# A second GpSimd drain in the last stage of an attention and mixture-of-experts kernel

## The chip, the cores and the metric

The kernel runs on one NeuronCore of a Trainium2 chip. The metric is the device time of one execution in microseconds. Before the change the median of three runs is 1449.51 us (1448.92 to 1450.37). Beside these stands one execution under the hardware profiler, from which all durations below come.

## What is computed

The reference is a post-norm transformer block over `x` of shape (4, 1024, 256): attention with 16 heads of size 16 and rotary-like position factors, a residual and a layer norm, then a mixture of 8 experts with top-2 routing and a capacity, a residual and a second layer norm. Only the second half matters here:

```python
logits = x_flat @ router_w + router_b
gates = softmax(logits)
_, topk_idx = top_k(gates, 2)
expert_mask = one_hot(topk_idx, 8).sum(1)
pos = cumsum(expert_mask, axis=0) - 1          # the token's slot within its expert
expert_mask = expert_mask * (pos < capacity)   # capacity = 640 slots for each of 8 experts
buf[e, pos] += x_flat                          # tokens are dispatched to slots
h = gelu(einsum('ecd,edh->ech', buf, w1) + b1[:, None, :])
out = einsum('ech,ehd->ecd', h, w2) + b2[:, None, :]
y = sum over e of out[e, pos] * gates
x = layernorm(x + y)
```

There are N = 4096 tokens of 256 features; an expert's hidden width is 1024.

## The kernel before

**Attention** takes the first 1130 us or so. It is a hand-written order of pieces over 32 units (batch, head group) and is not touched. While it runs, GpSimd scatters every finished token's row into the table `slots_in` in DRAM (L646), twice per tile of 128 tokens, one row for each of its two experts.

**The expert stage** begins at L1056. It is a loop over the experts `e` from 0 to 7 (L1206), within `tc.manual_schedule()`, so that the order of the source is the order of each engine's queue. An expert's 640 slots are five tiles of 128 (`ST` = 5). For each expert:

- SP loads the slots of the next expert (L1210), and the VectorE works out for the slots which token each belongs to, its gate, and three row numbers (`tokens_of`, L1085).
- GpSimd gathers five tiles of partial results that an earlier expert left for the same tokens (`others_of`, L1168, one indirect transfer per tile).
- If there was an expert before, its rows, which are now complete for those tokens that have no later expert, are normalized (`normalized`, L1220) and scattered to the output by GpSimd (`sent`, called at L1224, the transfer is L1191), one indirect transfer per tile. Rows that are not finished have a row number beyond the bounds and are skipped by the transfer.
- First layer: eight groups of four matmuls (L1230), each followed by a Gelu on ScalarE (L1237).
- Second layer: for each of the five tiles eight matmuls (L1249). For experts 0 to 6 the result is biased, weighted, added to the row and scattered to the table `y_rank` (L1267). For the last expert it is added to the row (L1257), the row is normalized by itself (L1260) and sent to the output at once (L1261, the transfer is again L1191).

All these indirect transfers are issued from GpSimd, which writes their descriptors itself; SP and ScalarE issue plain ones. GpSimd's queue is strictly in order. Each transfer signals its landing on one of eight semaphores in turn. `out_views` (L1188) gives the first tile of each expert a view of the whole output, so the scatter of the second tile waits for the landing of the first.

**The end of the program** is written by the framework when the `TileContext` closes, so it has the line L1344: SP waits for the last value of every semaphore, that is, for every landing and every engine. Then all five engines meet: each executes a `DRAIN` and signals, GpSimd waits for the other four, releases them, drains again, clears the semaphores, and there is a second meeting of the same kind. The program has no GpSimd drain between the meeting at its start (L1332) and this one.

Of the kernel before, what the change touches and what calls it, by code (L numbers as in the profile page):

```python
# [28 lines left out]
def kernel(  # L29
# [18 lines left out]
    nc = tc.nc  # L48
    B, S, DIM = x.shape
    E, _, HID = w1.shape  # L50
# [41 lines left out]
    def expert_weights(e):  # L92
        w_sb = big.tile([P, 4, S], F32, tag="big", name=f"w_{e}")
        w1_sb = w_sb[:, 0:2, :]
        nc.sync.dma_start(w1_sb, w1[e].rearrange("(k p) f -> p k f", p=P))
        w2_sb = w_sb[:, 2:4, :].rearrange("p k (c d) -> p (k c) d", d=DIM)
        nc.sync.dma_start(w2_sb, w2[e].rearrange("(k p) d -> p k d", p=P))
        return w1_sb, w2_sb
# [3 lines left out]
    with ExitStack() as actx:  # L102
# [869 lines left out]
        with tc.manual_schedule():  # L972
            for n in range(NS):
                u, c = divmod(n, NT)
                b, p = divmod(u, NU)
                if c == 0:
                    if u + 2 < B * NU:
                        load_qk(u + 2)
                    elif u + 2 - B * NU < 2:
                        e = u + 2 - B * NU  # L980
# [75 lines left out]
    with ExitStack() as mctx:  # L1056
# [12 lines left out]
        def slots_of(e):  # L1069
            s_sb = m2.tile([P, ST, ROW], F32, tag="slots", name=f"slots_{e}")  # L1070
            nc.sync.dma_start(
                s_sb, slots_in[e * CAP : (e + 1) * CAP, :].rearrange("(t p) d -> p t d", p=P)
            )
            return s_sb

        def transposed(e, s_sb, t):

            if t == 0:
                s_ts[e] = m2.tile([P, KC, CAP], F32, tag="slots_t", name=f"slots_t_{e}")
            ps = ps_t.tile([P, KC, P], F32, tag="t", name=f"st_{e}_{t}")  # L1080
            for k in range(KC):
                nc.tensor.transpose(ps[:, k, :], s_sb[:, t, k * P : (k + 1) * P], ident)
            nc.scalar.copy(s_ts[e][:, :, t * P : (t + 1) * P], ps)  # L1083

        def tokens_of(e, s_sb):  # L1085


            mine = m2.tile([P, 2, ST, 2], F32, tag="mine", name=f"mine_{e}")
            w = m2.tile([P, ST], F32, tag="w", name=f"w_{e}")
            gone = m2.tile([P, 3, ST], F32, tag="gone", name=f"gone_{e}")  # L1090
            to = m2.tile([P, 3, ST], U32, tag="to", name=f"rows_{e}")
            nc.vector.tensor_scalar(
                mine[:, 0], s_sb[:, :, DIM + 2 : DIM + 4], float(E - e), None, ALU.is_equal
            )
            nc.vector.tensor_tensor(mine[:, 1], mine[:, 0], s_sb[:, :, DIM : DIM + 2], ALU.mult)
            nc.vector.tensor_reduce(w, mine[:, 1], AX.X, ALU.add)
            nc.vector.tensor_reduce(gone[:, 0], mine[:, 0], AX.X, ALU.add)
            nc.vector.tensor_tensor(gone[:, 0], gone[:, 0], s_sb[:, :, DIM + 4], ALU.mult)
            nc.vector.tensor_scalar(gone[:, 0], gone[:, 0], -1.0, NOWHERE, ALU.mult, ALU.add)
            for i, k in ((1, 1), (2, 0)):  # L1100
                nc.vector.scalar_tensor_tensor(
                    gone[:, i], mine[:, 0, :, k], float(N), gone[:, 0], ALU.mult, ALU.add
                )

            nc.vector.tensor_scalar(gone[:, 2], gone[:, 2], 2.0 * N - 1.0, None, ALU.min)
            nc.vector.tensor_copy(to, gone)
            return w, to
# [44 lines left out]
        def without_experts(q):  # L1152


            t0 = q * NQ
            for t in range(t0, t0 + NQ):
                nc.vector.tensor_scalar(x1[:, t, :], x1[:, t, :], again[:, t : t + 1], None, ALU.mult)
            b, t = divmod(t0, NT)
            nc.sync.dma_start(
                out[b, t * P : (t + NQ) * P, :].rearrange("(t p) d -> p t d", p=P),  # L1160
                x1[:, t0 : t0 + NQ, :],
            )
# [27 lines left out]
        def sent(row, to, t):  # L1190
            nc.gpsimd.indirect_dma_start(  # L1191
                out=out_views[t],
                out_offset=bass.IndirectOffsetOnAxis(ap=to[:, 0, t : t + 1], axis=0),
                in_=row[:, t, :],
                in_offset=None,
                bounds_check=N - 1,
                oob_is_err=False,
            )
# [4 lines left out]
        with tc.manual_schedule():  # L1203
            for t in range(ST):
                transposed(0, tiles[0], t)
            for e in range(E):  # L1206
                w1_sb, w2_sb = experts.pop(e)
                s_sb, s_t = tiles.pop(e), s_ts.pop(e)
                if e + 1 < E:
                    tiles[e + 1] = slots_of(e + 1)  # L1210
                if e == 0:
                    for q in range(7, 3, -1):
                        without_experts(q)
                w, to = tokens_of(e, s_sb)
                others = others_of(e, s_sb, w, to)
                row = next(others)

                if before:
                    b_row, b_to = before
                    normalized([b_row[:, t, :] for t in range(ST)], f"e_{e}")  # L1220
                next(others, None)
                if before:
                    for t in range(ST):
                        sent(b_row, b_to, t)  # L1224
                h_t = m2.tile([P, HC, CAP], F32, tag="h", name=f"h_{e}")
                for c in range(HC):
                    ps = ps_h.tile([P, 2, 512], F32, tag="h", name=f"hp_{e}_{c}")
                    for k in range(KC):
                        for i in range(2):
                            nc.tensor.matmul(  # L1230
                                ps[:, i, 0:half],
                                w1_sb[:, k, c * P : (c + 1) * P],
                                s_t[:, k, i * half : (i + 1) * half],
                                start=(k == 0),
                                stop=(k == KC - 1),
                            )
                    nc.scalar.activation(  # L1237
                        h_t[:, c, :].rearrange("p (i n) -> p i n", i=2),
                        ps[:, :, 0:half],
                        AF.Gelu,  # L1240
                        bias=b1_sb[:, e, c : c + 1],
                    )
                for t in range(ST):
                    if e + 1 < E and t > 0:
                        for i in (t - 1,) if t < ST - 1 else (t - 1, t):
                            transposed(e + 1, tiles[e + 1], i)
                    ps = ps_o.tile([P, DIM], F32, tag="o", name=f"op_{e}_{t}")
                    for c in range(HC):
                        nc.tensor.matmul(  # L1249
                            ps,  # L1250
                            h_t[:, c, t * P : (t + 1) * P],
                            w2_sb[:, c, :],
                            start=(c == 0),
                            stop=(c == HC - 1),
                        )
                    if e == E - 1:
                        nc.vector.scalar_tensor_tensor(  # L1257
                            row[:, t, :], ps, w[:, t : t + 1], row[:, t, :], ALU.mult, ALU.add
                        )
                        normalized([row[:, t, :]], f"e_{e}_{t}", by_scalar=True)  # L1260
                        sent(row, to, t)  # L1261
                        continue
                    o_sb = m4.tile([P, DIM], F32, tag="o", name=f"o_{e}_{t}")
                    nc.vector.tensor_tensor(o_sb, ps, b2_sb[:, e, :], ALU.add)  # L1264
                    nc.scalar.activation(o_sb, o_sb, AF.Identity, scale=w[:, t : t + 1])  # L1265
                    nc.vector.tensor_tensor(row[:, t, :], row[:, t, :], o_sb, ALU.add)
                    nc.gpsimd.indirect_dma_start(  # L1267
                        out=y_views[e * ST + t],
                        out_offset=bass.IndirectOffsetOnAxis(ap=to[:, 1, t : t + 1], axis=0),
                        in_=o_sb,  # L1270
                        in_offset=None,
                        bounds_check=2 * N - 1,
                        oob_is_err=False,
                    )
                    if e == 0 and t < 4:
                        without_experts(3 - t)
                before = row, to
                if e + 2 < E:
                    experts[e + 2] = expert_weights(e + 2)
# [68 lines left out]
```

## Time and profile before

| | |
|---|---|
| median of 3 runs | 1449.51 us |
| the profiled execution, its time | 1455.47 us |
| the profiled execution, its span (first to last instruction) | 1453.6 us |
| granted TensorE clock, mean | 0.972 |
| busy: PE, VectorE, ScalarE, GpSimd | 94%, 63%, 50%, 28% of the span |
| indirect transfers from GpSimd | 64 (L646), 40 (L1191), 35 (L1267), 35 (L1168) |
| descriptor work of one L1191 transfer on GpSimd | 0.98 us in the median |
| distance of the last five L1191 transfers | 3.45 us |

The time of the profiled execution is 1.87 us longer than its span, and 5.96 us longer than the median of the runs. Times in the profile are counted from the first instruction. An entry with a `q` behind the engine's name (POOLq, SPq) was executed by that engine's queue and is not part of its busy time: waits, register moves, semaphore instructions and drains. The engine names PE, DVE, ACT and POOL stand for TensorE, VectorE, ScalarE and GpSimd.

### The profile page before, as it was taken

The page shows a single profiled execution, that of the slowest core. Times are in us where ns is not written, and L with a number is a line of the kernel's source. Part 1 is how long each engine was busy: PE and PEld are TensorE (multiplying, and loading weights), DVE is VectorE, ACT ScalarE, POOL GpSimd, SP SyncE. Part 2 cuts the span into 40 slices and gives each one's busy share as a digit, 9 for nine tenths or more (in the row PEclk, how much of TensorE's full clock was granted, in tenths as well). Part 3 has the DMA queues.
Part 4 walks back from the last instruction along what each step waited for, and adds up shares of the span by engine and source line. Part 5 has one row for each costly group of instructions (what it writes and reads, how often), then busy time and mean ns, then how long its engine had stood idle before and what let it go on. Part 6 is the DMA issues. An engine that isn't in the chain of part 4 may idle for free. (4 is left out here: it accounts for less than half of the span.)

```text
span 1453.6 us, 24361 instructions
## 1 busy us (share of the span) xinstructions
PE 1367.7 (94%) x9314; PEld 859.4 (59%) x9314; DVE 921.3 (63%) x1990; ACT 727.5 (50%) x944; POOL 411.2 (28%) x436
## 2 busy tenths in 40 slices
PE   5899999999999999999999999999996399999996
PEld 3455555655665565555555555555543277777775
DVE  7767766667877766787767677887644433333334
ACT  5365666565566556546674654655553122222221
POOL 5640043340002637000064530000210414444542
PEclk8899999999999999999999999999998599999998
DMA  7956367373444646454465352224210436433211
GB/s 240 261 177 173 100 188 205 87 228 107 126 120 113 213 133 180 121 151 102 129 185 181 105 176 74 63 63 118 90 64 0 139 112 212 115 120 131 73 44 43
DMA packets 107315, 191.23 MB, mean 132 GB/s; under 512 B 19633, under 2 KB 56178, under 8 KB 107072
## 3 DMA queue, kind: packets, MB, share of 16 engines
q1 hardware_dynamic: 96192, 167.80, 39.7%
q0 software_dynamic: 9888, 20.01, 4.5%
q10 hardware_dynamic: 1120, 1.87, 0.4%
q8 instruction: 73, 1.20, 0.4%
q14 instruction: 42, 0.34, 0.1%
HBM read 119.32 MB, written 73.63 MB: 133 GB/s over the span
## 5 line engine op out<-in xcount | busy, mean ns | idle before, releaser
L705 DVE TENSOR_REDUCE nm<-s 128x1 f32<-128x512 f32 x1024 | 644.8, 684 | 230.4 <-PE s L701 212.6
L750 ACT ACTIVATE pt<-st 128x1024 f32<-128x1024 f32 x512 | 496.3, 1021 | 393.7 <-PE st L743 378.9
L701 PE MATMUL s<-qk 128*128 128x512 f32 x1024 | 391.5, 441 | 25.6 <-DVE nm L705 14.5
L728 PE MATMUL st<-qk 128*128 128x512 f32 x1024 | 308.4, 401 | 3.5 <-ACT pt L750 3.4
L764 PE MATMUL av<-pt,va 128*32 128x256 f32 x4096 | 275.5, 386 | 0.5 <-ACT pt L750 0.5
L701 PEld LDWEIGHTS s<-qk 128*128 128x128 f32 x1024 | 180.2, 191 | 138.3 <-DVE nm L705 62.4
L728 PEld LDWEIGHTS st<-qk 128*128 128x128 f32 x1024 | 183.3, 189 | 67.1 <-ACT pt L750 32.7
L764 PEld LDWEIGHTS av<-pt,va 128*32 128x32 f32 x4096 | 107.1, 109 | 107.8 <-issue 62.4
L646 POOL DMA_INDIRECT slots_in<-held,scatter_idx x64 | 62.7, 980 | 304.4 <-DVE scatter_idx L644 226.4
L390 POOL TENSOR_TENSOR soft_q<-y_q,soft_q 128x512 f32<-128x512 f32 x14 | 17.9, 1282 | 447.3 <-ACT soft_q L386 447.2
L1249 PE MATMUL op<-w,h 128*128 128x256 f32 x640 | 144.1, 379 | 0.0
L1230 PE MATMUL hp<-slots_t,w 128*128 128x320 f32 x512 | 139.9, 434 | 0.0
L743 PE MATMUL st<-mt,ones_r 2*128 2x512 f32 x1024 | 129.6, 495 | 0.7 <-ACT mt L721 0.7
L1249 PEld LDWEIGHTS op<-w,h 128*128 128x128 f32 x640 | 119.4, 190 | 15.9
L1230 PEld LDWEIGHTS hp<-slots_t,w 128*128 128x128 f32 x512 | 97.7, 191 | 40.0 <-ACT slots_t L1083 0.3
L743 PEld LDWEIGHTS st<-mt,ones_r 2*128 2x128 f32 x1024 | 49.0, 181 | 89.5 <-issue 88.1
L1237 ACT ACTIVATE h<-hp,b_sb 128x640 f32<-128x640 f32 x64 | 50.8, 794 | 86.6 <-PE hp L1230 73.3
L1264 DVE TENSOR_TENSOR o<-op,b_sb 128x256 f32<-128x256 f32 x35 | 14.9, 425 | 93.3 <-PE op L1249 88.9
L1265 ACT ACTIVATE o<-o,w 128x256 f32<-128x256 f32 x35 | 17.8, 507 | 103.1 <-issue 71.9
L1267 POOL DMA_INDIRECT y_rank<-o,rows x35 | 35.9, 1025 | 98.4 <-ACT slots_t L1083 42.2
L1191 POOL DMA_INDIRECT out_dram<-row,rows x40 | 41.0, 1025 | 44.6 <-DVE row L1146 14.3
L396 POOL TENSOR_TENSOR e_k<-soft_k,tab_k 128x512 f32<-128x512 f32 x28 | 35.4, 1286 | 46.3 <-DMA tab_k<-table 45.8
(210 smaller groups left out, 1030.6 us busy)
## 6 DMA issues: line engine op xcount, KB each, us to landing
qk<-embed_q SPq DMA_DIRECT2D x248, 128.0 KB
qk<-embed_k SPq DMA_DIRECT2D x124, 256.0 KB
embed_k<-parts_k SPq DMA_DIRECT2D x64, 256.0 KB
w<-in_w_dram SPq DMA_DIRECT2D x16, 1024.0 KB
embed_q<-parts_q SPq DMA_DIRECT2D x56, 256.0 KB
y_rank<-zero SPq DMA_DIRECT2D x8, 1024.0 KB
tab_k<-table SPq DMA_DIRECT2D x14, 512.0 KB
tab_q<-table SPq DMA_DIRECT2D x12, 512.0 KB
```

The source lines that it names most:

```text
L646: nc.gpsimd.indirect_dma_start(out=scatter_views[2 * t + k], out_offset=bass.IndirectOffsetOnAxis(ap=scatter_idx[:, k, t : t + 1], axis=0) ...
L701: nc.tensor.matmul(ps, qk[:, 2 * h, lo : lo + P], qk[:, 2 * h + 1, j * HS : (j + 1) * HS], start=True, stop=True,)
L705: nc.vector.tensor_reduce(nms[u][:, j, i, s : s + 1], ps, AX.X, ALU.max, negate=True)
L728: nc.tensor.matmul(ps[:, f, :], qk[:, 2 * h + 1, c * P : (c + 1) * P], qk[:, 2 * h, f * HS : (f + 1) * HS], start=True, stop=False,)
L743: nc.tensor.matmul(tiles[h][:, f, :], ones_r[rows, :], mts[u][rows, :], start=False, stop=True,)
L750: nc.scalar.activation(pt, tiles[h], AF.Exp)
L764: nc.tensor.matmul(av[32 * s : 32 * (s + 1), cols], va[f][:, c, 2 * p + h, :], pt[h][:, s // 2, cols], start=(c == 0 and n == 0), stop=(c ...
L1191: nc.gpsimd.indirect_dma_start(out=out_views[t], out_offset=bass.IndirectOffsetOnAxis(ap=to[:, 0, t : t + 1], axis=0), in_=row[:, t, :], i ...
L1230: nc.tensor.matmul(ps[:, i, 0:half], w1_sb[:, k, c * P : (c + 1) * P], s_t[:, k, i * half : (i + 1) * half], start=(k == 0), stop=(k == KC ...
L1237: nc.scalar.activation(h_t[:, c, :].rearrange("p (i n) -> p i n", i=2), ps[:, :, 0:half], AF.Gelu, bias=b1_sb[:, e, c : c + 1],)
L1249: nc.tensor.matmul(ps, h_t[:, c, t * P : (t + 1) * P], w2_sb[:, c, :], start=(c == 0), stop=(c == HC - 1),)
L1267: nc.gpsimd.indirect_dma_start(out=y_views[e * ST + t], out_offset=bass.IndirectOffsetOnAxis(ap=to[:, 1, t : t + 1], axis=0), in_=o_sb, in ...
```

## The change

In the last pass of the expert loop, behind the five scatters of expert 6's rows and in front of the first layer of expert 7, a `drain` is put on GpSimd's queue. It carries no wait and signals nothing. It is the same kind of instruction that the framework puts there at the end.

```diff
                 if before:
                     for t in range(ST):
                         sent(b_row, b_to, t)
+                if e == E - 1:
+
+                    nc.gpsimd.drain()
                 h_t = m2.tile([P, HC, CAP], F32, tag="h", name=f"h_{e}")
                 for c in range(HC):
                     ps = ps_h.tile([P, 2, 512], F32, tag="h", name=f"hp_{e}_{c}")
```

Because of the three added lines, later lines have numbers that are higher by three in the changed kernel: L1344 becomes L1347, L1257 becomes L1260. L1191 keeps its number, and the drain is L1227.

## The prediction

> **What bounds the kernel now.** I read the page from the bottom of the program upwards, since the added instruction stands some 27 us before the end. First the page itself: its span, the queue of GpSimd's transfers (software_dynamic) and the chain.
>
> ```profile
> span 1453.6 us, 24361 instructions
> ...
> q0 software_dynamic: 9888, 20.01, 4.5%
> ...
> POOL out_dram L1191 0%; POOLq L1344 0%; DMA out_dram<-row,rows 0%; POOLq L1191 0%
> ```
>
> TensorE is busy for 94% of the span, so nothing on GpSimd (28%) matters before the last matmuls; what counts is what stands behind them. The same chain in order of time ends so:
>
> ```profile
> 1441.08 0.97 POOL out_dram L1191
> 1442.06 2.25 issue
> 1444.30 1.21 POOLq L1344
> ```
>
> The last piece stops at 1445.51, with the last scatter (issued from 1444.54 for 0.97). But the span is 1453.6. The chain says nothing of the last **8.1 us**, because instructions that only a queue executes are not counted as work. The listing of the closing line L1344 (duration min/median/max in ns, first and last start), first whole, then for the windows 1444 to 1446 and 1452.8 to 1453.05, and the opening drain of L1332, fill the hole:
>
> ```profile
> L1344 POOLq DRAIN  x3: 51/93/8553, 1444.3 to 1453.4; - x3
> L1344 SPq DRAIN  x3: 7/7/7, 1447.3 to 1453.1; - x3
> ```
> ```profile
> L1344 POOLq DRAIN  x1: 8553/8553/8553, 1444.3 to 1444.3; - x1
> ```
> ```profile
> L1344 POOLq EVENT_SEMAPHORE  x2: 17/17/17, 1452.9 to 1453.0; - x2
> ```
> ```profile
> L1332 POOLq DRAIN  x1: 169/169/169, 0.3 to 0.3; - x1
> ```
>
> One GpSimd drain runs from 1444.30 to 1452.85. SP, which waits for every landing, is through at 1447.3; then everything waits for GpSimd. Is anything moving in that time? The busy times by stretch (stretch, length, then busy us and count of PE, PEld, DVE, ACT, POOL, clock, DMA share, GB/s), and the DMA row of the window 1445.6 to 1453.6, where a digit is 0.2 us:
>
> ```profile
> 1445.52:1453.60 8.08, 0.00 (x0) 0.00 (x0) 0.00 (x0) 0.00 (x0) 0.00 (x0) 0.50 0.05 16
> ```
> ```profile
> DMA  0079100000000000000000000000000000000000
> DMA packets 48, 0.13 MB, mean 16 GB/s; under 512 B 16, under 2 KB 16, under 8 KB 48
> ```
>
> Nothing: the last 48 packets (one scatter) are over by about 1446.6. So 1452.85 - 1445.51 = **7.34 us** of that drain lie behind the last descriptor work, and at least 6.2 us behind the last packet. The program's end is bound by a GpSimd drain that waits for no data.
>
> **The change, part by part.** It adds one such drain on GpSimd's queue, behind the fifth scatter L1191 of expert 6's rows and before the five scatters of expert 7's. No other engine gets, loses or moves an instruction, and no wait or transfer is changed; the instruction order shows that the GpSimd queue differs by this one entry. Two terms follow: what the added drain costs where it stands, and what it takes from the last one.
>
> *Term 1, the added drain in its place.* GpSimd's own timeline there:
>
> ```profile
> 1425.32 0.98 POOL L1191 DMA_INDIRECT out_dram<-row,rows  x1 [0.30 <-issue]
> 1430.72 0.97 POOL L1191 DMA_INDIRECT out_dram<-row,rows  x1 [4.42 <-DVE row L1146]
> 1434.18 0.97 POOL L1191 DMA_INDIRECT out_dram<-row,rows  x1 [2.48 <-DVE row L1146]
> 1437.63 0.97 POOL L1191 DMA_INDIRECT out_dram<-row,rows  x1 [2.48 <-DVE row L1146]
> 1441.08 0.97 POOL L1191 DMA_INDIRECT out_dram<-row,rows  x1 [2.48 <-DVE row L1146]
> 1444.54 0.97 POOL L1191 DMA_INDIRECT out_dram<-row,rows  x1 [2.48 <-DVE row L1146]
> ```
>
> The drain can work from 1426.30, when the fifth scatter's descriptors are written. Its lower end is the wait for the last landing, 1.5 us (the queue's wait for that transfer is passed at 1427.8 already in this trace): that lies inside the idle 4.42 us and costs nothing. The nearest row for the upper end is the closing drain, 7.34 us: it ends at 1433.64. Queued behind it are only the five scatters of expert 7; nobody waits for these but SP at the very end (their rows are not reused). With 0.3 us for issue the first starts at 1433.9, not 1430.72, 3.2 us late. The second must wait for the first to land; at L1191 earlier (1417.98, next 1421.24) that distance is 3.26: 1437.2. The third follows 1.28 later (0.98 + 0.30): 1438.5 instead of 1437.63; the fourth could start at 1439.7 but its row comes at 1441.08 as before. So the delay is eaten up by the fourth, because the scatters come every 3.45 us (PE's eight matmuls and the normalization) and need only 1.28. The last one stays at 1444.54: **cost 0**. The cover ends when the first scatter starts after 1444.54 - 3.26 - 3 x 1.28 = 1437.4, that is, with a drain longer than about 10.8 us; from there each us counts fully.
>
> *Term 2, the closing drain.* What it does in 7.34 us the trace doesn't show, only what sets it: the drain at the start, with no transfer behind it, takes 0.17 us, and the two that follow the long one 0.09 and 0.05. It is paid for transfers made since the last drain, either (a) by their number or (b) once per drain, as soon as there are any. Lower end of the gain, (b): 0. Upper end, (a): by the issue rows GpSimd starts 64 + 40 + 35 + 35 indirect and 8 + 16 + 12 plain transfers, 210; 5 of these stand behind the added drain. The estimate 7.34 x 5/210 = 0.17 us (by packets 5 x 48 / 9888 = 2.4%, the same) leaves the closing drain done by about 1445.7, or, if it waits for the landing first, by 1447.2. Then SP is late next: its drain at 1447.3 meets the barrier. From the long drain's end to the span's end it takes 1453.6 - 1452.85 = 0.75 us of barrier and semaphore clearing. New end: 1447.3 + 0.05 + 0.75 = 1448.1. **Gain 1453.6 - 1448.1 = 5.5 us.** Of the two I take (a). 7.3 us with no packet moving and no engine at work is software going through something; 7.34 us / 210 = 35 ns per transfer is a plausible pace for bookkeeping, while a fixed procedure of 7 us would be odd beside drains of 0.05 us.
>
> **Two rules against the row.** The Trainium skill, "PSUM — Partial Sum Buffer", Engine vs sequencer instructions, says that a drain waits until its engine is fully idle, and no more. By that rule the closing drain would end with the last scatter at 1445.5, SP at 1447.3 would already bound the end, and the change would be worth 0. The row has 7.34 us beyond idleness. And "VectorE: DVE Perf Modes", The DRAIN you can't avoid, knows the surrounding drains as constant, about 12 ns on all five engines: by it a further one costs nothing and saves nothing. The row here agrees for SP (7 ns) but has 8553 ns for GpSimd. I go by the row; the rules' answer, 1449.5, is the same number as (b).
>
> **From the profiled execution to the median.** Profiled it took 1455.47 us with a span of 1453.6, so 1.87 lie around the span; the runs' median is 1449.51, 5.96 less. I take the gain over in us: 1455.47 - 5.5 = 1450.0 profiled, 1449.51 - 5.5 = **1444.0** for the runs. That the tail is as long without the profiler is an assumption.
>
> **The rivals.**
> - *Fixed price (b), no change, 27%.* Each drain with transfers behind it costs 7.3 us. For it: the trace has one drain with transfers, so no slope is seen; a poll over the DMA rings would look the same. Against it: the argument above. The added drain stays hidden, the closing one stays: 1449.5. The case that the added drain returns at once and does nothing belongs here, as does a tail that exists only under the profiler.
> - *A part of each, faster, 6%.* A fixed base of some 3 us and the rest by number: the closing drain ends at 1445.5 + 3.1 = 1448.6, 4.2 us sooner: 1445.3.
> - *The added drain outlasts its cover, slower, 7%.* Place: GpSimd's queue before the scatter of 1430.72. Here DVE, PE and other DMAs are at work, which they are not behind 1445.5. If that stretches it to twice 7.34 = 14.7 us, it ends at 1441.0; the scatters start at 1441.3 and the last at 1448.4. If the closing drain also keeps its fixed 7.34, the end is 1449.4 + 7.34 + 0.75 = 1457.5, 3.9 later: 1453.4. It decides only beyond 10.8 us, and only if (b) holds too: with a closing drain that gets short, the same stretch would still end before 1453.6.
>
> **How the numbers follow.** By number (a): 60%, 1443.3 to 1445.5 on its own (the runs spread by 1.4 us). Within 0.2% (2.9 us, about what this kernel's measurement can tell from none) lies only the fixed price. Faster 0.60 + 0.06 and some of what I can't name, 0.65; same 0.28; slower 0.07. The range must reach the fixed price to leave out less than 2 in 10: 1443.3 to 1450.3.
>
> **What would show it.** In the changed profile: a POOLq DRAIN at the added line of some 7 us from about 1426 (term 1; if it is 0.1 us, nothing was due there); the scatters of expert 7 late at first and on time from the fourth; a closing drain under 3 us and a span near 1448.1 (term 2). A closing drain still near 8.5 us makes (b) right. A last scatter later than 1444.5 means that the cover was too short.

## The result and the profile after

Over 22 runs of each kernel the changed one takes 0.9958 of the time of the one before (95% interval 0.9949 to 0.9967): 1446.17 us in the median against 1451.68, 6.1 us by the ratio's middle and 4.8 to 7.4 by its ends. The forecast was 1444.0 us where the kernel before took 1449.51, a ratio of 0.9962. The kernel before ran 2 us slower in these runs than in its first three, so the ratio counts and not the forecast's absolute time.

The closing line has the number L1347 now. Its listing and that of the added drain (duration min/median/max in ns, first and last start in us) in the changed kernel:

```profile
L1347 POOLq DRAIN  x3: 51/93/2885, 1439.6 to 1443.1; - x3
L1347 SPq DRAIN  x3: 7/7/7, 1442.6 to 1442.9; - x3
```
```profile
L1227 POOLq DRAIN  x1: 10795/10795/10795, 1418.1 to 1418.1; - x1
```

The listed time of the closing drain shrank from 8.55 to 2.89 us, and it ends at 1442.51. SP is through with its waits at 1442.6, so the two now meet at the barrier, where before SP, through at 1447.3, had to wait for GpSimd until 1452.85, 5.5 us. The time went to the added drain, which ends at 1428.85. How it lies among GpSimd's transfers shows in the timeline of the changed kernel (start, duration, what, and in brackets the idle time before and what ended it):

```profile
1420.93 0.97 POOL L1191 DMA_INDIRECT out_dram<-row,rows  x1 [0.30 <-issue]
1429.88 0.97 POOL L1191 DMA_INDIRECT out_dram<-row,rows  x1 [7.97 <-DVE row L1146]
1433.09 0.97 POOL L1191 DMA_INDIRECT out_dram<-row,rows  x1 [2.23 <-DVE row L1146]
1434.36 0.97 POOL L1191 DMA_INDIRECT out_dram<-row,rows  x1 [0.30 <-DVE bs_e L1121]
1436.41 0.97 POOL L1191 DMA_INDIRECT out_dram<-row,rows  x1 [1.07 <-DVE row L1146]
1439.86 0.97 POOL L1191 DMA_INDIRECT out_dram<-row,rows  x1 [2.48 <-DVE row L1146]
```

GpSimd's idle time before the scatter of 1429.88 is 7.97 us, put down to the VectorE; in truth it is the drain, since the VectorE had written that row by 1425.77:

```profile
1425.36 0.41 DVE L1146 TENSOR_SCALAR row<-row,mv_e,root_e 128x256 f32<-128x256 f32 x1
```

The scatters follow at distances of 3.21, 1.27, 2.05 and 3.45 us: late, catching up, on time from the fourth.

The profiled span fell by more, 1453.6 to 1443.4 = 10.2 us. Only half of that is the change. The first matmul group of the first expert and the last tell the parts (PE timeline, before):

```profile
1156.76 1.79 PE L1230 MATMUL hp<-slots_t,w 128*128 128x320 f32 x3
...
1406.75 17.39 PE L1230 MATMUL hp<-slots_t,w 128*128 128x320 f32 x64
```

and in the changed kernel, where the line is L1233:

```profile
1151.68 1.81 PE L1233 MATMUL hp<-slots_t,w 128*128 128x320 f32 x3
...
1402.07 2.32 PE L1233 MATMUL hp<-slots_t,w 128*128 128x320 f32 x8
```

Attention, to which nothing was done, came out 5.1 us shorter in this execution. Over the profiles of all kernels here without extra transfers the first expert starts between 1150.6 and 1156.8, so a single execution can't be read for less than some 6 us there. From the last expert's first matmul to the end it is 1453.65 - 1406.75 = **46.90** us before and **41.33** after: 5.57 us, where the forecast had 5.5. This stretch varies little (41.32 to 41.33 in three kernels with a drain at the place of the change), and the experiments below are read by it.

### The profile page after: what moved, and what is told of

Read it like the earlier page. It is cut to its first block, busy times and chain, and to the rows that moved or that the text cites. A ratio compares the mean times of both kernels' runs of the same rounds, so it can differ in the third digit from the quotient of the medians.

```text
span 1443.4 us, 24362 instructions
## 1 busy us (share of the span) xinstructions
PE 1364.8 (95%) x9314; PEld 858.3 (59%) x9314; DVE 920.0 (64%) x1990; ACT 727.3 (50%) x944; POOL 410.5 (28%) x436
## 5 line engine op out<-in xcount | busy, mean ns | idle before, releaser
L1233 PE MATMUL hp<-slots_t,w 128*128 128x320 f32 x512 | 140.3, 435 | 0.0
L1233 PEld LDWEIGHTS hp<-slots_t,w 128*128 128x128 f32 x512 | 98.0, 192 | 40.2 <-issue 0.4
L1191 POOL DMA_INDIRECT out_dram<-row,rows x40 | 41.3, 1032 | 44.9 <-DMA out_dram<-row,rows 14.4
L463 DVE TENSOR_TENSOR held<-po,held 128x512 f32<-128x512 f32 x32 | 22.1, 690 | 41.6 <-PE po L455 41.6
```

Of the source, the lines that this page charges most:

```text
L1191: nc.gpsimd.indirect_dma_start(out=out_views[t], out_offset=bass.IndirectOffsetOnAxis(ap=to[:, 0, t : t + 1], axis=0), in_=row[:, t, :], i ...
L1233: nc.tensor.matmul(ps[:, i, 0:half], w1_sb[:, k, c * P : (c + 1) * P], s_t[:, k, i * half : (i + 1) * half], start=(k == 0), stop=(k == KC ...
```

## The experiments

Where no ratio is given, a run is one profiled execution. The price of a drain is counted from the end of GpSimd's last work in front of it to the end of the drain, since the queue enters the drain while that work is still running. In the change the fifth scatter's descriptors are written at 1420.93 + 0.97 = 1421.90 and the drain ends at 1428.85, so its price is 6.94 us. A transfer has landed when its data have arrived and its semaphore says so. Before the runs I held that the price goes by the number of transfers since the last drain, 35 ns each; the rival was a price paid once for all by the first drain.

**Four drains.** One more behind the transfers of the start, one behind attention, one as in the change:

```diff
             load_qk(0, halves[1], "q", nc.gpsimd)
+            nc.gpsimd.drain()
...
             run(one)
+            nc.gpsimd.drain()
             nc.scalar.preload_act_table_set("gelu_and_others")
...
+                if e == E - 1:
+                    nc.gpsimd.drain()
                 h_t = m2.tile([P, HC, CAP], F32, tag="h", name=f"h_{e}")
```

> Three drains are added: behind the 36 plain transfers of the start, behind the 64 scatters of attention, and before the last expert's first layer as in the change; the closing one stays. The price of a drain is counted from the end of the descriptor work in front of it. By number of transfers since the last drain (35 ns each): 36 -> 1.3 us (or the 1.5 us of a landing, if that is longer), 64 -> 2.2 us, 105 -> 3.7 us, 5 -> the landing alone, 1.5 to 1.7 us. If instead the first drain after transfers pays once and for all (something is loaded or set up once): about 7 us at the start and 1.5 to 1.7 us at each of the three others. If each drain has a fixed price: about 7 us at all four.

The listings of its four places, in order:

```profile
L940 POOLq DRAIN  x1: 7105/7105/7105, 40.8 to 40.8; - x1
```
```profile
L1054 POOLq DRAIN  x1: 11800/11800/11800, 1137.2 to 1137.2; - x1
```
```profile
L1228 POOLq DRAIN  x1: 12462/12462/12462, 1418.6 to 1418.6; - x1
```
```profile
L1348 POOLq DRAIN  x3: 46/97/2875, 1440.2 to 1443.7; - x3
```

Less the work that was still running, 6.22 us for 36 transfers, 5.30 for 64, 8.63 for 105 and 1.67 for 5. Nothing is paid once for all, nor is the price fixed: both rivals fall. But my 35 ns falls with them: 64 and 105 transfers cost more than twice of it, 82.8 and 82.2 ns each. The 36 of the start are a case by themselves: the last packet of these ends only at 45.40, in the middle of heavy loads (another queue's packets take 87% of the DMA engines' time there), 2.5 us before the drain's end at 47.90. The run's stretch at the end is 41.32 us, that of the change: at this place a price of 8.63 us is hidden as well as one of 6.94.

**One drain, behind attention.** Of the three only the second is kept.

> One drain only, behind attention's last scatter, none before the last expert. By number: it pays for 100 transfers (3.5 us), and the closing drain for the 110 since then: 3.9 us behind the last scatter, so the end comes 3.5 us sooner than before: ratio 0.9976. A once-for-all price: 7 us at the drain, 1.5 to 1.7 us at the end, ratio 0.996 as the change. Fixed price: closing drain 7.3 us, ratio 1.000. If the drain holds up the first expert's loads, up to 0.002 has to be added.

The listings of the added drain and of its closing line:

```profile
L1053 POOLq DRAIN  x1: 14738/14738/14738, 1135.4 to 1135.4; - x1
```
```profile
L1345 POOLq DRAIN  x3: 46/97/10246, 1438.7 to 1449.4; - x3
```

The added drain takes 8.24 us for 100 transfers, the closing one 9.04 for 110: 82 ns each again, where the expectation had 3.5 and 3.9 us. So with fewer transfers behind it (110 instead of 210) the closing drain takes *longer* than before, 9.04 against 7.35, and the last stretch is 48.59 us. The ratio, 1.0007 (0.9991 to 1.0024), agrees with those 1.7 us (1.0012) and with no change alike; the stretch decides. A drain put in the wrong place gains nothing.

**A drain in each pass.** `if e > 0:` in place of `if e == E - 1:`.

> A drain at the change's place in each of the passes 1 to 7. By number: the first pays for 115 transfers, 4.0 us, and each of the others for 15, 0.5 us, so not more than the landing in front of it, 1.5 us; the closing one 1.5 to 1.7 us. All lie under TensorE's work: ratio as the change, 0.996. A once-for-all price: 7 us in the first, 1.5 us in the others, same ratio. If drains in a row cost cover that the gathers and scatters of the next expert need: slower than the change, over 0.997.

The listing of its seven drains:

```profile
L1226 POOLq DRAIN  x7: 5087/5426/13193, 1214.0 to 1429.3; - x7
```

The first, with 115 transfers, has a price of 9.47 us (82.3 ns each); the six others, with 15 (1.24 us at that rate), 1.77 to 2.68; in the longest of these the last packet ends only 1.6 us behind the descriptor work. And the first outlasts its cover. GpSimd's next scatter and what hangs on it (timeline of this kernel; its lines are two higher than before):

```profile
1228.09 0.97 POOL L1269 DMA_INDIRECT y_rank<-o,rows  x1 [10.40 <-issue]
...
1234.94 0.42 DVE L1266 TENSOR_TENSOR o<-op,b_sb 128x256 f32<-128x256 f32 x1 [10.04 <-DMA y_rank<-o,rows]
1235.44 0.51 ACT L1267 ACTIVATE o<-o,w 128x256 f32<-128x256 f32 x1 [10.47 <-DVE o L1266]
...
1236.69 1.44 PE L1232 MATMUL hp<-slots_t,w 128*128 128x320 f32 x2 [5.10 <-ACT h L1239]
```

The scatters to `y_rank` hold the four buffers of `o`; the VectorE has to wait for one, ScalarE for the VectorE, and the Gelu that TensorE needs stands behind that on ScalarE. The passes before the last expert take 258.68 us against 250.39 in the change, 8.3 more; the end keeps its 41.33. Of these 8.3 us TensorE waits for 5.10. The rest goes with a lower granted clock behind that wait (stretch, length, then busy us and count of PE, PEld, DVE, ACT, POOL, clock, DMA share, GB/s):

```profile
1236.69:1240.00 3.31, 3.31 (x6) 2.18 (x7) 3.04 (x18) 0.63 (x1) 0.56 (x1) 0.50 0.04 8
1240.00:1245.00 5.00, 5.00 (x15) 3.40 (x14) 3.86 (x19) 1.59 (x2) 3.12 (x4) 0.75 0.19 52
```

At 0.50 for 3.31 us and 0.75 for 5.00 the loss is 2.9 us (an estimate from these two lines); in the change the clock was 1.00 in the same part of the pass. Measured: ratio 1.0017 (1.0005 to 1.0029), **slower** than before although the closing drain is as short as in the change. This is the last of the prediction's rivals, at another place and by another path: the delay goes through buffers that TensorE's chain needs.

**A drain with little cover.** The drain stands behind the fourth of the last expert's five scatters:

```diff
                         sent(row, to, t)
+                        if t == 3:
+                            nc.gpsimd.drain()
                         continue
```

> The added drain stands behind the fourth of the last expert's five scatters, where only 2.5 us of cover are left. My theory (the drain is only moved under cover by the change): it takes 7.3 us from about 1442.1, the last scatter starts near 1449.7 instead of 1444.5, the closing drain then takes 1.7 us, and the span ends about 0.5 us earlier than before: ratio 0.9996, 0.999 to 1.001. If a drain in the middle helped for another reason than its place (an earlier stage that got faster, as the profiled executions might suggest): as the change, 0.996.

The last two scatters in GpSimd's timeline of this kernel:

```profile
1438.20 0.97 POOL L1191 DMA_INDIRECT out_dram<-row,rows  x1 [2.48 <-DVE row L1146]
1447.24 0.97 POOL L1191 DMA_INDIRECT out_dram<-row,rows  x1 [8.07 <-issue]
```

Price 7.27 us for 209 transfers. The last scatter starts 9.04 us behind the fourth instead of 3.45, the closing drain takes 1.53 behind it, and the stretch is 46.92 us, before's 46.90 (0.5 less was expected); ratio 1.0004 (0.9987 to 1.0020). The same drain out of its cover is worth nothing: what the change gains by is the place.

These runs left a contradiction: 64, 100, 105, 110 and 115 transfers all cost 82 ns each, while 205, 209 and 210 cost 6.94, 7.27 and 7.35 us. The differences within the second group fit the same rate (0.41 us for 5), but 205 x 82.4 ns would be 16.9. Some 121 transfers are missing. The other runs went after these.

**The drain of pass 2.** `if e == 2:`, one drain, with 130 transfers behind it and 80 to come.

> The one drain of the change, but in the pass of expert 2, where 130 transfers lie behind it. With 121 taken off: 9 x 82.4 ns, so the landing alone, 1.5 to 2 us; the closing drain then has 80: 6.6 us, 0.75 us less than before: ratio 0.9995. With nothing taken off so early: 10.7 us in pass 2, which is more than the cover that pass 1 had, so TensorE stalls by some 8 us: ratio over 1.004.

The listings of the added and of the closing drain:

```profile
L1226 POOLq DRAIN  x1: 3410/3410/3410, 1249.9 to 1249.9; - x1
```
```profile
L1346 POOLq DRAIN  x3: 51/92/7796, 1441.5 to 1449.8; - x3
```

1.54 us for 130 transfers, which is a landing alone (1.53 us for the single transfer of the run before), and 6.59 for 80 (82.4 ns each). Set beside the full price of the 115 in the run with a drain in each pass, the loss happens between the 115th and the 130th transfer, without a drain. Nor is there a pause of the 10 us that 121 transfers would cost: between these two GpSimd's longest gap is 5.9 us. The stretch is 46.13, 0.77 less than before as expected; the ratio, 0.9998 (0.9986 to 1.0010), can't tell that from nothing.

**Forty more transfers, no drain.** Plain transfers of zeros to an unused table, of 128 rows of 1 KB each, in attention's third batch:

```diff
+        waste = dram.tile([40, 128, 256], F32, name="waste")
+
+        def wasted(i):
+            nc.gpsimd.dma_start(waste[i], zero[0:128, 0:256])
...
+        for i in range(40):
+            at(2, i // NT, i % NT, wasted, i)
```

> No drain is added; 40 more plain transfers of 128 rows from GpSimd in batch 2 of attention, so that the closing drain has 250 behind it. If a count of about 121 transfers is taken off each time it is reached: 250 - 242 = 8, the closing drain takes the landing alone (1.5 to 1.7 us) and the kernel is as fast as the change without any drain, ratio 0.996. If it was taken off once only, by something in the expert stage: 7.35 + 40 x 0.0824 = 10.6 us, ratio 1.002. If plain transfers in attention don't count: 7.35 us, ratio 1.000.

The listing of its closing line:

```profile
L1352 POOLq DRAIN  x3: 46/93/3635, 1447.2 to 1451.3; - x3
```

With *more* transfers the closing drain has less to do: 2.43 us, and the stretch is 42.26 us, 4.6 less than before. It is not the 8 transfers that I expected to be left but 2.43 / 0.0824 = 29.5. The ratio is 0.9996 (0.9983 to 1.0009) all the same. The first expert starts at 1159.6 here. In the four profiles with extra transfers it starts at 1156.8 to 1159.6, in the seven without at 1150.6 to 1156.8, 5.1 us earlier in the mean. So the gain at the end was probably paid for in attention, where the extra transfers are issued; that is argued, not shown.

**Forty small ones,** the same with `zero[0:1, 0:256]`, one row each, without and with a drain in pass 2 (one profile each):

> As the run with forty more transfers, but each of one row of 1 KB instead of 128. No drain is added; 250 transfers lie behind the closing one. If what is taken off on the way is a number of transfers (106 to 121 each time): about 30 are left, 2.4 us, as with the forty large ones. If it is a full table whose places are used up by the pieces of a transfer, not by the transfer (a one-row transfer then fills it by less, an estimate of a quarter of a large one): the first loss comes later and is larger, about 150 transfers, no second one follows, and about 100 are left: 8 us.

> The same forty one-row transfers and in addition the one drain in the pass of expert 2, which has 170 behind it. If a number of transfers is taken off: 170 - (106 to 121) = 49 to 64, 4 to 5.3 us there, and 80 x 82.4 ns = 6.6 us at the end. If it is a full table: about 150 off, 20 left, so the landing or little more, 1.5 to 2 us, and 6.6 us at the end. If nothing has been taken off yet by then: 14 us.

The listing of the closing line without a drain, and of the added drain in the other kernel:

```profile
L1352 POOLq DRAIN  x3: 51/93/3636, 1444.9 to 1449.1; - x3
```
```profile
L1234 POOLq DRAIN  x1: 7763/7763/7763, 1250.5 to 1250.5; - x1
```

The closing drain takes 2.43 us behind its last scatter, to the hundredth what it took with the large ones: a transfer counts as one, whatever its rows, and the theory of a table filled by a transfer's pieces falls. In pass 2, with 170 behind it, the drain has a price of 4.08 us = 49.5 transfers at 82.4 ns, so 120.5 were taken off, as with 205 to 210. The 80 that follow cost 6.59 again.

**Small and large ones between drains,** 64 of each:

```diff
+        def wasted(i, rows):
+            nc.gpsimd.dma_start(waste[i, 0:rows], zero[0:rows, 0:256])
...
+        for b, rows in ((2, 1), (3, 128)):
+            at(b, 0, 0, nc.gpsimd.drain)
+            for i in range(64):
+                at(b, i // 16, i // 2 % NT, wasted, 64 * (b - 2) + i, rows)
+            at(b, 4, 0, nc.gpsimd.drain)
```

> Adds 128 plain transfers of zeros from GpSimd into an unused DRAM table, 64 of one row of 1 KB in batch 2 and 64 of 128 such rows in batch 3, each set between two drains; five prices in one profile. The runs so far fit 82.4 ns per transfer since the last drain. By transfers: 52 in front of the first drain 4.3 us, the 64 one-row ones 5.3, 16 scatters 1.3 (so the landing, 1.5 or more), the 64 of 128 rows 5.3. By rows or descriptors: the one-row ones cost the landing alone, 1.5 to 2 us, the others as before. The closing drain has 142 transfers: 82.4 ns x (142 - 121) = 1.7 us if a backlog of about 121 transfers is taken off on the way, as 205, 209 and 210 transfers suggest; 11.7 us if not.

The first and the third of the four added drains, with 52 and with 16 transfers behind them, and the work in front of the third:

```profile
L1024 POOLq DRAIN  x1: 6785/6785/6785, 584.1 to 584.1; - x1
```
```profile
L1024 POOLq DRAIN  x1: 3835/3835/3835, 850.7 to 850.7; - x1
```
```profile
850.58 2.53 POOL L405 TENSOR_TENSOR parts_k<-e_k,parts_k 128x512 fp32r<-128x512 f32 x2
```

The 52 cost 4.34 us (83 ns each) and the 16 cost 1.39 (87 ns each), counted from the end of the vector work in front. I had expected a landing, 1.5 us or more, for the 16. But here nothing was left to land: the last packet of the 16 ends at 808.89, 44 us before the price begins at 853.11, and with the 52 it is 44 us as well. So the price goes by the number even where all has long arrived, and time that passes before the drain doesn't lessen it. The 64 of one row cost 6.02 and the 64 of 128 rows 7.59, both above the expected 5.3; they were issued in bursts, and their last packets end 2.4 and 4.3 us behind the last issue, so these two prices hold more than the rate. Behind the last packet 3.6 and 3.3 us are left, where a single transfer has 0.44: a one-row transfer is not nearly free. The closing drain took 3.01 us for 142 transfers, 36.5 of them: 105.5 taken off and not 121. How many go, and when, is thus not one number: 120.5 the first time in each run without an earlier drain, another 100 by the end of the runs with 250, 105.5 here. What does it stays open.

## Why the prediction was right, and where it was not

*What bounds the end.* Right: the closing drain did, and beyond the last packet. With it shortened, SP's last landing and the barrier are left, and the stretch at the end is 5.57 us shorter where 5.5 was forecast.

*Term 1.* Right: cost 0, the first scatter late, the fourth and fifth on time. The drain took 6.94 us (forecast 7.34 as the upper end). The step from the drain's end to the first scatter took 1.03 us and not the 0.3 put in, so counted from TensorE's last first layer that scatter is 3.8 us late instead of 3.2, and the cover nearer 10 us than 10.8. What was luck is that the price lay within it. I compared 7.34 us with the 10.8 that the place could hold, but the price behind 205 transfers is 6.94 only because 121 had dropped out; at 82.4 ns each, all 205 would be 16.9 us, 6 to 7 us over the cover and so more than the whole gain (an estimate from these runs). In pass 1, with 115 transfers, the same instruction did outlast its cover. The rival to which I gave 7% was nearer than that.

*Term 2.* The gain is right to 0.1 us in the last stretch, and the choice of (a), by number, over (b) was right too. What work it is stays open: that it is software, as I argued, no run shows. The term that was mis-sized is its rate: 7.34 us / 210 = 35 ns per transfer is an average over a count of which 121 no longer counted. The rate is 82.4 ns on what is left. For this change it made no difference, because 5 transfers at either rate (0.17 or 0.41 us) lie below the landing, and the closing drain took the 1.68 us of that; for a drain elsewhere it decides, as the run with the drain behind attention shows, where the forecast from 35 ns was 3.9 us and 9.04 came.

*The two rules.* The row decided rightly against both, as I had read them. A GpSimd drain is not over when the last work that the profile counts as busy ends: with 110 transfers behind it, it took 9.04 us beyond. Whether GpSimd is idle in the sense of the first rule in that time, no run shows, and that a drain does no more than wait for it was my addition. As to the second rule, SP's drains are 7 ns; the closing drain of GpSimd was 8553.

*From profile to runs.* The ratio agrees with the assumption that the tail is as long without the profiler: 4.8 to 7.4 us hold the 5.57 of the trace.

## What to carry to other kernels

Where a kernel starts transfers from GpSimd, look at the GpSimd drain on the program's last line: it is not in the chain of waits, and it can hold the end for microseconds in which nothing moves. A drain placed where GpSimd's queue is free for longer than its price moves that work under cover; put it as late as the cover allows, since only the transfers behind it are left for the end. Read the cover from who waits for the transfers queued behind it: the same instruction was free in the last pass, and in the second it cost TensorE 5.1 us of waiting and some 3 us at a lower clock. And take the price from a profile of the kernel at hand, since the number of transfers alone doesn't give it.

## What was not expected of the hardware

- Up to 115 transfers, a GpSimd drain costs some 82.4 ns for each that GpSimd has started since the last drain (1.39 us for 16, 5.30 for 64, 9.47 for 115). This holds where the transfers had landed 44 us before. Where the last has just been issued, it costs no less than that landing (1.5 to 1.7 us). Transfers of one row and of 128 rows count alike (2.43 us with forty of either).
- Of a longer series 100 to 121 transfers drop out of this without any drain, so that the price is a sawtooth: 9.47 us for 115 transfers, 1.54 for 130, 7.35 for 210, 2.43 for 250. What takes them off is not known.
